# A mixture-of-experts block's second routing loop: tokens four to a partition, whole-row stores, shared experts in pieces, late counts

## The chip, the cores and the metric

The kernel runs on one core of one Trainium2 chip. The metric is device time in microseconds, from the start to the end of one execution; a kernel's time is the median of its runs. A core has TensorE (PE; loading of its weights is shown as PEld), VectorE (DVE), ScalarE (ACT), GpSimd (POOL) and SyncE (SP), each with its own stream of instructions that it works through in order. Engines wait for each other and for transfers through semaphores. DMA transfers are issued by SP, ACT and POOL; an instruction that waits at the head of a stream holds up everything behind it on that engine.

## The reference

The input x has 16 x 512 = 8192 tokens of width 256. Four parts follow each other, each on layer-normalised input and added to x: softmax attention (16 heads), a mixture of experts, a gated linear attention ("forget" attention), and the same mixture of experts again. All is float32. The mixture of experts is:

```python
logits = x.astype(jnp.float32) @ router_w.T          # 64 experts
probs = jax.nn.softmax(logits, axis=-1)
topk_w, topk_ids = jax.lax.top_k(probs, K)           # K = 8
topk_w = topk_w / jnp.sum(topk_w, axis=-1, keepdims=True)
...
pos = jnp.cumsum(onehot, axis=0)[jnp.arange(N), flat_e] - 1
valid = pos < C                                      # C = 128 places an expert
...
g = jnp.einsum('ecd,edf->ecf', xb, w_gate)           # F = 192
u = jnp.einsum('ecd,edf->ecf', xb, w_up)
h = jax.nn.silu(g) * u
y = jnp.einsum('ecf,efd->ecd', h, w_down).reshape(E * C, -1)
...
gu = x @ ws_gate_up                                  # the shared expert, F = 192
sg, su = (gu[:, :SF], gu[:, SF:])
shared = jax.nn.silu(sg) * su @ ws_down
return routed + shared
```

An expert takes its first 128 tokens in token order and drops the others, so the running count of tokens for each expert, over all 8192 tokens in order, decides what is computed.

## The kernel before

The tokens are cut into 16 blocks of 512, a block into four chunks of 128. The first mixture of experts is routed inside the attention's schedule; the second has a loop of its own, in `Block.routed(part, loads=True)`. `Part` holds what both share. The order of the instructions on each engine is written out by hand (`manual_schedule`): an engine works in the order in which the Python code issues.

**The second layer's loop** (L1268 on) runs over b from -4 to 16, each step working on several blocks. In step b it loads block b+4 (SP), chooses the experts of block b, normalises block b+2, transposes block b+1, runs the shared expert's gate and up matmuls and its silu for block b-3, computes router logits and the softmax's numerators for b+1, counts block b, sends the shared expert's result for b-4 through its down matmuls, and takes the moments (mean and variance) for b+3. In detail:

- `normed` (L1530) stores a normalised block's 256 columns to `rows` in DRAM; `choose` (L1575) divides by the softmax's sum (L1579 to L1581), finds the eight largest values of each token (L1589, L1590), makes a mask of them, and stores 64 expert weights per token into the last columns of the same rows. A row of `rows` has 320 values.
- `count` (L1606) transposes the mask with four matmuls (L1611) and copies it out of PSUM (L1613). `added` (L1615) makes the running count with one scan on VectorE (L1619) that begins with the last block's end, and stores it to `counts` in DRAM. `counted` (L1506) reads it back into `cw`, chunks on partitions. The last block goes straight from chip to chip (`straight`, L1512), with two of four DMAs issued by SP and two by ACT.
- `gu` (L1628), `chunk` (L1636) and `silu` (L1647) are the shared expert's first half, `down` (L1677) its second, in two halves; the second half stores the block's result from SP. A matmul in float32 stands as two rows in the trace.
- Expert weights come in pairs of experts, four DMAs a pair (`fetch`, L1483); five pairs are fetched in steps 2 to 6 of the loop, four pieces in a step. Eleven pairs fit on chip.

**The tail.** After the loop `chunks_before` (L1070) reads the counts, and `find` (L1079), driven by `place`, finds each expert's 128 tokens in five pieces of work; the first two calls handle two experts each, the later ones four. Between the pieces stand the shared expert's matmuls for the last blocks. `gather` (L1133) gets the rows of the found tokens by an indirect DMA from POOL.

**The experts.** For each expert the loop at L1359 gathers the rows of six experts ahead, transposes (`turned`), multiplies (`widened`, `narrowed`), and adds the result to `out` or `routed` by an indirect DMA with addition from POOL (L1200), alternating. Weight pieces of later pairs are issued at an even pace. Before it, `part.own.close()` releases the loop's buffers, and `part.slots` zeroes the padding of the new weight buffers on POOL (L1480), which waits for the last readers of the released memory.

At the end `joined` adds `routed` to `out` with eight DMAs of 1 MB.

Of the kernel before, what the change touches and what calls it, by code (L numbers as in the profile page):

```python
# [37 lines left out]
class Block:  # L38
# [131 lines left out]
    def attention(self, x, x1, wqkv, wo, rope, part, later):  # L170
# [14 lines left out]
        with ExitStack() as c:  # L185
# [271 lines left out]
            def each(s):  # L457
# [9 lines left out]
                    if b + far < z - 2 or work not in expert  # L467
# [556 lines left out]
    def routed(self, part, loads=False):  # L1024
# [9 lines left out]
        with ExitStack() as c:  # L1034
# [6 lines left out]
            if loads:  # L1041
                part.look_up("right")
                part.slots(5, "right")
            else:
                part.slots(4, "right")
# [13 lines left out]
            def load(b):  # L1059
                xs[b] = p3.tile([P, CB, D], F32, name="x")  # L1060
                nc.sync.dma_start(
                    out=xs[b], in_=x[ts(b, BLK), :].rearrange("(c p) d -> p c d", p=P)
                )
# [63 lines left out]
            accs = (x, y)  # L1127
# [56 lines left out]
            def narrowed(e):  # L1184
# [3 lines left out]
                for m in range(2):  # L1188
# [12 lines left out]
                    out=accs[e % 2],  # L1201
# [10 lines left out]
            with tc.manual_schedule(  # L1212
# [8 lines left out]
                nb, lag, ahead = self.nblk, 3, 6  # L1221
# [33 lines left out]
                def counts(b):  # L1255
                    part.added(b, stored=b < nb - 1)
                    (part.counted if b < nb - 1 else part.straight)(b)

# [8 lines left out]
                if loads:  # L1267
                    for b in range(-4, nb + 1):  # L1268
# [6 lines left out]
                        run(b - lag, nb, gu)  # L1275
                        run(b - lag, nb, silu)
# [3 lines left out]
                        run(b, nb, counts)  # L1280
                        run(b - 1 - lag, nb, down)
                        run(b + 1, nb, part.exps)
                        run(b + 3, nb, lambda b: part.moments(b, xs[b]))
                        if 2 <= b < 7:
                            fetch(b - 2)
                        if b == nb:
                            chunks_before()
                            place(0, 3)

                    begun, done, z = 5, 0, nb - 1  # L1290
# [3 lines left out]
                    part.gu(z - 1, 0)  # L1294
                    place(2, 1)
                    part.gu(z - 1, 1)
                    place(2, 1)
                    gather_to(3)
                    silu(z - 1)
                    part.down(z - 2, 0)  # L1300
                    part.down(z - 2, 2)
                    place(4, 3)
                    part.gu(z, 0)
                    place(4, 1)
                    part.gu(z, 1)
                    place(4, 1)
                    gather_to(5)
                    silu(z)
                    down(z - 1)
                    down(z)  # L1310
# [43 lines left out]
                part.own.close()  # L1354
                part.slots(part.pairs - len(part.slot), "left")

                rest = [(n, piece) for n in range(begun, E // 2) for piece in range(4)]
                due, last = len(rest), E - 10
                for e in range(done - 2, E):  # L1359
                    if e + ahead > 5:  # L1360
                        run(e + ahead, E, gather_to)
# [4 lines left out]
                    run(e, E, narrowed)  # L1366
                    while rest and (due - len(rest)) * last < due * (e + 1):
# [31 lines left out]
ROOMY = dict(xn=2, xnT=5, pr=2, rest=2, chosen=2, wt=2, cs=2, cum=2, th=2, hT=2, y=2)  # L1399


class Part:
# [6 lines left out]
    def __init__(self, ctx, k, x, y, weights, room, pairs, side):  # L1409
        rw, self.w_gate, self.w_up, self.w_down, ws_gu, ws_down = weights  # L1410
        self.ctx, self.pairs, self.slot, self.ws = ctx, pairs, [], {}
        self.k, self.nc, self.x, self.y, self.room = k, k.nc, x, y, room
# [23 lines left out]
        self.end = 0.0  # L1436
# [3 lines left out]
    def begin(self, queue):  # L1440
        rw, ws_gu, ws_down = self.shared_weights
        nc, T, w = self.nc, self.k.T, self.pools[1]
        self.rw_sb = w.tile([P, KD, E], F32, name="rw_sb")
        queue.dma_start(out=self.rw_sb, in_=rw.rearrange("(k p) f -> p k f", p=P))
# [13 lines left out]
        for i in range(self.room["hT"]):  # L1458
            hT = w.tile([P, 2, BLK], F32, name=f"hT{i}")
            nc.gpsimd.memset(hT[FT:P, 1, :], 0.0)  # L1460
            self.hidden.append(hT)
        for z in (self.rows, self.x, self.y):
            queue.dma_start(out=z[T : T + P, :], in_=self.k.zeros[:, 0 : z.shape[1]])

# [47 lines left out]
    def straight(self, b):  # L1512

        for i in range(CB):
            at, queue = b * CB + i, (self.nc.sync, self.nc.scalar)[i % 2]
            queue.dma_start(out=self.cw[at : at + 1], in_=self.cum[:, ts(i, P)])
# [5 lines left out]
    def here(self, b):  # L1522
        return self.rows[ts(b, BLK), :].rearrange("(c p) d -> p c d", p=P)
# [6 lines left out]
    def normed(self, b, xt):  # L1530
        mv, va, yy = self.mvs.pop(b)
        rstd = self.k.refined(va, yy)
        self.xns[b] = self.tile("xn", [P, CB, D])
        self.k.normed(self.xns[b], xt, mv, rstd, 0)
        self.nc.sync.dma_start(out=self.here(b)[:, :, 0:D], in_=self.xns[b])

    def features(self, b, pool=None):
        xn = self.xns.pop(b)
# [36 lines left out]
    def choose(self, b, piece):  # L1575
        nc, small, pr = self.nc, self.k.small, self.prs[b]
        if piece == 0:
            sm = small.tile([P, CB], F32, name="sm")
            nc.vector.tensor_reduce(sm, pr, AX.X, ALU.add)  # L1579
            nc.vector.reciprocal(sm, sm)  # L1580
            nc.vector.tensor_tensor(  # L1581
                pr, pr, sm.unsqueeze(2).to_broadcast([P, CB, E]), ALU.mult
            )
# [14 lines left out]
        wt = self.tile("wt", [P, CB, E])  # L1598
# [4 lines left out]
        nc.sync.dma_start(out=self.here(b)[:, :, D:ROW], in_=wt)  # L1603
        del self.prs[b], self.tops[b], self.rests[b]

    def count(self, b):  # L1606
# [6 lines left out]
        self.nc.scalar.copy(self.csums[b], cT[0:E, :])  # L1613
# [32 lines left out]

    def silu(self, b, piece):  # L1647
        if piece == 0:
            self.hTs[b] = self.hidden[b % len(self.hidden)]
# [7 lines left out]
    def gate(self, b):  # L1657
# [3 lines left out]
        self.hTs[b] = self.hidden[b % len(self.hidden)]  # L1661
# [15 lines left out]
    def down(self, b, i, pool=None):  # L1677
# [3 lines left out]
        py = self.bank()  # L1681
        for k in range(2):
# [130 lines left out]
```

## Time and profile before

| what | us |
|---|---|
| median of 3 runs (2653.41 to 2655.82) | 2655.49 |
| the profiled execution | 2652.72 |
| its span, first to last instruction | 2650.8 |
| first layer's scatters | 1424.2 to 1643.6 |
| forget attention ends (last addition) | 2131.9 |
| first moments of the second loop | 2142.3 |
| count scans 0, 13 and 15 of the second loop | 2162.23, 2324.39, 2341.03 |
| counts read on chip (L1071) | 2352.08 |
| first scatter of the second layer | 2386.09 |
| last scatter | 2601.34 |
| final addition issued | 2605.76 |

All times in a trace are from the first instruction of the span. The granted clock is TensorE's, 1 being full speed. In a line of the timeline stand the start, the duration, the engine, the source line, the operation, what it writes and reads by the program's names, the shapes, and the number of instructions merged into the line; in brackets the idle time of the engine just before, and what ended it. An engine name with a q is its sequencer issuing a DMA. In a line of waits: who waited for whom, then the total, the number of times and the longest, in us.

### The profile page before, as it was taken

The page shows a single profiled execution, that of the slowest core. Times are in us where ns is not written, and L with a number is a line of the kernel's source. Part 1 is how long each engine was busy: PE and PEld are TensorE (multiplying, and loading weights), DVE is VectorE, ACT ScalarE, POOL GpSimd, SP SyncE. Part 2 cuts the span into 40 slices and gives each one's busy share as a digit, 9 for nine tenths or more (in the row PEclk, how much of TensorE's full clock was granted, in tenths as well). Part 3 has the DMA queues.
Part 4 walks back from the last instruction along what each step waited for, and adds up shares of the span by engine and source line. Part 5 has one row for each costly group of instructions (what it writes and reads, how often), then busy time and mean ns, then how long its engine had stood idle before and what let it go on. Part 6 is the DMA issues. An engine that isn't in the chain of part 4 may idle for free.

```text
span 2650.8 us, 47730 instructions
## 1 busy us (share of the span) xinstructions
PE 2429.4 (92%) x17864; PEld 1514.1 (57%) x17864; DVE 1850.9 (70%) x4677; ACT 1333.9 (50%) x2750; POOL 844.4 (32%) x835
## 2 busy tenths in 40 slices
PE   7999999999999999999997886899999969998871
PEld 3444555555555555555446775567777656667771
DVE  6566677766777676776646664789889869867650
ACT  1566666666666666666542332466666523323330
POOL 3122212222221222212015775332322122117773
PEclk8899999999999999999898898899999969999996
DMA  1000111001110011100158896202111058739987
GB/s 57 1 10 27 35 37 35 14 29 35 37 35 14 29 35 37 36 20 13 35 146 231 222 240 151 82 30 64 54 53 53 22 148 187 177 105 263 246 224 148
DMA packets 210003, 226.47 MB, mean 85 GB/s; under 512 B 34286, under 2 KB 202222, under 8 KB 208750
## 3 DMA queue, kind: packets, MB, share of 16 engines
q1 hardware_dynamic: 180366, 174.43, 22.9%
q0 software_dynamic: 25728, 46.15, 8.8%
q8 instruction: 142, 2.33, 0.4%
q10 hardware_dynamic: 3680, 2.85, 0.3%
q14 instruction: 87, 0.71, 0.1%
HBM read 146.50 MB, written 84.48 MB: 87 GB/s over the span
## 4 chain that ended last, share of the span: by engine, by line
PE 75%; DVE 9%; DMA 8%; issue 3%; POOL 2%; ACT 1%; SPq 0%; POOLq 0%; ACTq 0%; DVEq 0%
PE sc L334 20%; PE sc L384 9%; DMA xe<-rows,token 4%; PE sc L260 4%; PE pb L811 4%; PE sc L1639 3%; PE sc L323 3%; PE sc L843 2%; PE pb L875 2%; PE sc L407 2%; PE sc L304 2%; PE sc L1684 2%; PE pb L920 2%; PE pb L736 2%; PE pb L1165 2%
## 5 line engine op out<-in xcount | busy, mean ns | idle before, releaser
L348 DVE TENSOR_REDUCE mx<-sc 128x1 f32<-128x512 f32 x1024 | 635.1, 682 | 296.2 <-PE sc L334 296.2
L374 ACT ACTIVATE pT<-sc 128x512 f32<-128x512 f32 x1024 | 527.9, 603 | 109.7 <-PE sc L334 109.7
L334 PE MATMUL sc<-qT,kT 17*128 17x512 f32 x2048 | 314.8, 647 | 0.0
L334 PE MATMUL sc<-kT,qT 16*128 16x512 f32 x2048 | 301.8, 610 | 0.3 <-DVE mx L348 0.3
L384 PE MATMUL sc<-pT,v 128*32 128x512 f32 x2048 | 244.3, 620 | 0.0
L104 POOL TENSOR_SCALAR va<-mv 128x4 f32<-128x4 f32 x64 | 14.7, 230 | 704.9 <-DVE mv L98 692.7
L860 DVE SCALAR_TENSOR_TENSOR pT<-sc,of,left 128x256 f32<-128x256 f32 x512 | 204.9, 472 | 21.7 <-PE sc L843 20.4
L334 PEld LDWEIGHTS sc<-kT,qT 16*128 16x128 f32 x2048 | 151.3, 190 | 91.5 <-issue 36.4
L282 POOL TENSOR_TENSOR t<-qk,rope_sb 128x512 f32<-128x512 f32 x62 | 78.8, 1270 | 382.1 <-ACT qk L268 374.5
L334 PEld LDWEIGHTS sc<-qT,kT 17*128 17x128 f32 x2048 | 94.0, 184 | 128.5 <-issue 95.6
L384 PEld LDWEIGHTS sc<-pT,v 128*32 128x32 f32 x2048 | 61.9, 113 | 174.4 <-issue 124.3
L1135 POOL DMA_INDIRECT xe<-rows,token x128 | 130.3, 1018 | 91.0 <-DVE token L1117 38.5
L144 ACT COPY oT<-sc 128x512 f32<-128x512 f32 x64 | 37.5, 586 | 172.7 <-PE sc L384 172.7
L260 PE MATMUL sc<-wqkv_sb,feat 128*128 128x512 f32 x256 | 124.4, 611 | 0.0
L811 PE MATMUL pb<-feat,wqk_sb 128*128 128x512 f32 x256 | 117.7, 593 | 0.0
L1200 POOL DMA_INDIRECT routed<-ye,token x64 | 102.7, 1605 | 40.9 <-DMA routed<-ye,token 10.8
L323 PEld LDWEIGHTS sc<-ident,pad 128*128 128x128 f32 x512 | 55.4, 144 | 104.4 <-ACT pT L374 81.9
L96 DVE BATCH_NORM_STATS2 bn<-x 128x6 f32<-128x256 f32 x256 | 89.0, 410 | 17.1 <-DMA x<-out 13.9
L1599 POOL TENSOR_TENSOR wt<-pr,chosen 128x256 f32<-128x256 f32 x32 | 23.3, 728 | 242.9 <-DVE chosen L1594 218.5
L1639 PE MATMUL sc<-xnT,wsg_sb 128*128 128x512 f32 x192 | 92.5, 608 | 0.0
L323 PE MATMUL sc<-ident,pad 128*128 128x128 f32 x512 | 87.0, 293 | 5.1 <-POOL pad L298 2.8
L290 POOL TENSOR_TENSOR t<-qk,rope_sb 128x256 f32<-128x256 f32 x124 | 90.7, 753 | 0.0
(225 smaller groups left out, 4897.9 us busy)
## 6 DMA issues: line engine op xcount, KB each, us to landing
ws<-in_w_gate SPq DMA_DIRECT2D x64, 384.0 KB
ws<-in_w_up SPq DMA_DIRECT2D x64, 384.0 KB
rows<-xn SPq DMA_DIRECT2D x32, 512.0 KB
routed<-y SPq DMA_DIRECT2D x32, 512.0 KB
ws<-in_w_down SPq DMA_DIRECT2D x64, 256.0 KB
x<-in_x SPq DMA_DIRECT2D x16, 512.0 KB
attended<-x SPq DMA_DIRECT2D x16, 512.0 KB
ws<-in_w_down SPq DMA_DIRECT2D x64, 128.0 KB
```

The costliest lines, as they stand in the source:

```text
L260: nc.tensor.matmul(pq, lhsT=xnTs[b][:, kd, ts(i, P)], rhs=wqkv_sb[:, kd, 0 : 2 * D], start=(kd == 0), stop=(kd == KD - 1),)
L290: eng.tensor_tensor(t2[:, :, lo : lo + HD // 2], qk2[:, :, :, 1 - half], rope_sb[:, i, HD + lo : HD + lo + HD // 2] .unsqueeze(1) .to_broa ...
L323: nc.tensor.transpose(pt[:, ts(i, P)], pads[b % 2][i][:, at : at + 4, :].rearrange("p h d -> p (h d)"), self.ident,)
L334: nc.tensor.matmul(scs[j], lhsT=lhs[at : at + high, ts(i, P)], rhs=rhs[at : at + high, :], start=True, stop=True,)
L348: nc.vector.tensor_reduce(mxs[n][:, j, i : i + 1], sc, AX.X, ALU.max, negate=True)
L374: nc.scalar.activation(pT[:, j, :], sc, AF.Exp, scale=float(HD) ** -0.5)
L384: nc.tensor.matmul(pav[ts(j, HP), :], lhsT=vs[b % 2][:, i, 4 * hg + j, :], rhs=pT[:, j, :], start=(i == 0), stop=(i == CB - 1),)
L811: nc.tensor.matmul(pq, lhsT=wqk_sb[:, kd, ts(m, P)], rhs=xnTs[b][:, kd, :], start=(kd == 0), stop=(kd == KD - 1),)
L860: nc.vector.scalar_tensor_tensor(pTs[n][:, :, ts(s8, HD)], sc[:, :, ts(s8, HD)], of[:, s8 : s8 + 1], here, ALU.mult, ALU.mult,)
L1135: nc.gpsimd.indirect_dma_start(out=xes[e], out_offset=None, in_=rows, in_offset=bass.IndirectOffsetOnAxis(ap=token[:, e : e + 1], axis=0),)
L1200: nc.gpsimd.indirect_dma_start(out=accs[e % 2], out_offset=bass.IndirectOffsetOnAxis(ap=token[:, e : e + 1], axis=0), in_=ye, in_offset=No ...
L1639: self.nc.tensor.matmul(to, lhsT=self.wsg_sb[:, kd, ts(m, P)], rhs=self.xnTs[b][:, kd, :], start=(kd == 0), stop=(kd == KD - 1),)
```

## The change

Only the second layer gets the new layout (`whole=True`); the first layer keeps its order of tokens.

- *Layout.* A partition holds four tokens in a row (`(p c) d -> p c d`) and no longer every 128th token (`(c p) d`), so a block's loads and stores move 4 KB in one piece per partition. `count` copies the counts back into token order by a strided write.
- *Rows whole.* A block's normalised values and its expert weights lie in one buffer of 320 columns, and are stored by one DMA after `choose`. Four such buffers are kept.
- *Softmax sum.* The three VectorE instructions that divide by the sum are removed, in both layers: the chosen weights are divided by their own sum afterwards, so it cancels.
- *Shared experts in pieces.* A block's work has cost 10: the first part (gate and up, 128 wide) 4, the second (64 wide) 2, each half of down 2. `shares` issues pieces up to a quota that grows evenly with b, beginning with block 0 in step 0. 140 of 160 units are due by the end of the loop, 10 before the counts are read, 10 between the placing steps.
- *Counts late.* Block b-1's counts are read back in step b. All four DMAs of the last block are issued by ACT, in both layers.
- *Queues and weights.* The second layer's shared results are stored from ACT. Four pairs of weights are fetched ahead, two pieces in a step from step 3 on; ten pairs fit on chip.
- *Unused here.* Blocks whose shared expert would be put off into the expert loop (`put_off`, `between`, `paid`) are set to none in both layers, so that code issues nothing.

```diff
-                part.slots(5, "right")
+                part.slots(4, "right")
+                part.queue = nc.scalar
...
-                    for b in range(-4, nb + 1):
+                    pieces = []
+                    for n, b in enumerate([*own, None]):
+                        if b is not None:
+                            pieces.append((4, b, first_part, b))
+                        if n > 0:
+                            pieces.append((2, own[n - 1], part.down, own[n - 1], 0))
+                            pieces.append((2, own[n - 1], part.down, own[n - 1], 2))
+                        if b is not None:
+                            pieces.append((2, b, second_part, b))
+                    total, spent = 10 * len(own), 0
+                    begun, done = 4, 0
+                    early = [(n, piece) for n in range(begun) for piece in range(4)]
+
+                    def shares(upto, newest=nb):
+                        nonlocal spent
+                        while pieces and spent + pieces[0][0] <= upto and pieces[0][1] <= newest:
+                            cost, _, work, *args = pieces.pop(0)
+                            spent += cost
+                            work(*args)
+
+                    for b in range(-4, nb):
                         run(b + 4, nb, load)
...
-                        run(b - lag, nb, gu)
-                        run(b - lag, nb, silu)
+                        shares((total - 20) * (b + 1) // nb, b)
                         run(b + 1, nb, part.logits)
                         run(b + 1, nb, part.likely)
                         run(b, nb, part.count)
-                        run(b, nb, counts)
-                        run(b - 1 - lag, nb, down)
+                        run(b, nb, lambda b: part.added(b, stored=b < nb - 1))
+                        if b == nb - 1:
+                            part.straight(b)
+
+                        run(b - 1, nb - 1, part.counted)
                         run(b + 1, nb, part.exps)
                         run(b + 3, nb, lambda b: part.moments(b, xs[b]))
-                        if 2 <= b < 7:
-                            fetch(b - 2)
...
+                        for _ in range(2):
+                            if b >= 3 and early:
+                                part.fetch(*early.pop(0))
+                    shares(total - 10)
+                    chunks_before()
+                    place(0, 3)
+                    shares(total - 8)
                     place(0, 2)
                     gather_to(1)
                     place(2, 3)
...
+                    shares(total - 6)
+                    place(2, 2)
                     gather_to(3)
...
                     place(4, 3)
+                    shares(total - 4)
+                    place(4, 2)
                     gather_to(5)
+                    shares(total)
...
-ROOMY = dict(xn=2, xnT=5, pr=2, rest=2, chosen=2, wt=2, cs=2, cum=2, th=2, hT=2, y=2)
+ROOMY = dict(xn=4, xnT=5, pr=2, rest=1, chosen=2, cs=2, cum=2, th=2, hT=2, y=2)
...
     def straight(self, b):
         for i in range(CB):
-            at, queue = b * CB + i, (self.nc.sync, self.nc.scalar)[i % 2]
-            queue.dma_start(out=self.cw[at : at + 1], in_=self.cum[:, ts(i, P)])
+            at = b * CB + i
+            self.nc.scalar.dma_start(out=self.cw[at : at + 1], in_=self.cum[:, ts(i, P)])
...
+    def tokens(self, z, b):
+        order = "(p c) d -> p c d" if self.whole else "(c p) d -> p c d"
+        return z[ts(b, BLK), :].rearrange(order, p=P)
...
-            sm = small.tile([P, CB], F32, name="sm")
-            nc.vector.tensor_reduce(sm, pr, AX.X, ALU.add)
-            nc.vector.reciprocal(sm, sm)
-            nc.vector.tensor_tensor(
-                pr, pr, sm.unsqueeze(2).to_broadcast([P, CB, E]), ALU.mult
-            )
...
-        nc.sync.dma_start(out=self.here(b)[:, :, D:ROW], in_=wt)
+        if self.whole:
+            nc.sync.dma_start(out=self.here(b), in_=row)
+        else:
+            nc.sync.dma_start(out=self.here(b)[:, :, D:ROW], in_=wt)
...
-        self.nc.scalar.copy(self.csums[b], cT[0:E, :])
+        if self.whole:
+            self.nc.scalar.copy(
+                self.csums[b].rearrange("e (p c) -> e c p", c=CB),
+                cT[0:E, :].rearrange("e (c p) -> e c p", c=CB),
+            )
+        else:
+            self.nc.scalar.copy(self.csums[b], cT[0:E, :])
...
-        part = Part(c, k, out, routed, moe, ROOMY, 11, "left")
+        part = Part(c, k, out, routed, moe, ROOMY, 10, "left", (), True)
```

## The prediction

> **What bounds the kernel now.** The page's engine line says only that TensorE is busy most of the time, so I went to the stretch table, cut at the borders of the stages: second layer's routing loop (2135 to 2341), its tail (to 2386), the experts (to 2601), the final addition.
>
> ```profile
> PE 2429.4 (92%) x17864; PEld 1514.1 (57%) x17864; DVE 1850.9 (70%) x4677; ACT 1333.9 (50%) x2750; POOL 844.4 (32%) x835
> ...
> 2135.00:2160.00 25.00, 12.52 (x52) 10.62 (x52) 13.74 (x61) 2.81 (x6) 6.05 (x10) 0.51 0.59 187
> 2160.00:2183.00 23.00, 16.97 (x66) 13.18 (x67) 22.03 (x81) 5.41 (x12) 5.30 (x9) 0.50 0.75 137
> 2183.00:2260.00 77.00, 73.24 (x331) 50.14 (x330) 71.73 (x240) 24.84 (x48) 15.66 (x24) 0.98 0.85 192
> 2260.00:2341.00 81.00, 74.74 (x344) 53.09 (x343) 73.50 (x247) 25.53 (x48) 15.74 (x24) 0.96 0.64 154
> 2341.00:2386.00 45.00, 42.54 (x177) 29.30 (x176) 23.63 (x53) 11.77 (x24) 10.02 (x13) 0.96 0.33 97
> 2386.00:2601.00 215.00, 179.95 (x1216) 158.92 (x1215) 136.20 (x382) 71.37 (x186) 159.50 (x120) 0.97 0.89 231
> ```
>
> After the stretch's length come PE, PEld, DVE, ACT and POOL, the granted clock, DMA share and GB/s. In the loop VectorE is full and TensorE nearly so; in the tail TensorE alone is. Next the timelines of the two engines through one iteration:
>
> ```profile
> 2217.61 1.04 PE L1545 MATMUL pb<-ident,xn 128*128 128x128 f32 x8
> 2218.49 5.32 PE L1639 MATMUL pb<-xnT,wsg_sb 128*128 128x512 f32 x12
> 2223.64 1.89 PE L1554 MATMUL pb<-rw_sb,xnT 128*128 128x64 f32 x16
> 2225.51 0.63 PE L1611 MATMUL pb<-ident,chosen 128*64 128x128 f32 x4
> 2225.97 3.62 PE L1684 MATMUL pb<-wsd_sb,hT 128*128 128x256 f32 x16
> 2229.43 1.04 PE L1545 MATMUL pb<-ident,xn 128*128 128x128 f32 x8
> ```
> ```profile
> 2219.36 1.27 DVE L1619 TENSOR_TENSOR_SCAN cum<-cs,cum 64x512 f32<-64x512 f32 x1
> ...
> 2222.12 0.38 DVE L1579 TENSOR_REDUCE sm<-pr 128x4 f32<-128x256 f32 x1
> 2222.54 0.18 DVE L1580 RECIPROCAL sm<-sm 128x4 f32<-128x4 f32 x1
> 2222.75 0.42 DVE L1581 TENSOR_TENSOR pr<-pr,sm 128x256 f32<-128x256 f32 x1
> 2223.21 0.23 DVE L1589 MAX8 top<-pr 128x8 f32<-128x64 f32 x1
> ...
> 2231.92 1.27 DVE L1619 TENSOR_TENSOR_SCAN cum<-cs,cum 64x512 f32<-64x512 f32 x1
> ...
> 2262.72 1.41 DVE L96 BATCH_NORM_STATS2 bn<-x 128x6 f32<-128x256 f32 x4 [4.18 <-DMA x<-out]
> ```
>
> From scan to scan VectorE takes 12.56 us, TensorE 11.82 from start to start. The queues' waits show why a load came late once:
>
> ```profile
> SPq L1508 <- DMA counts<-cum: 65.5, 15, 6.5
> ```
>
> SP sits behind each count store; once, at 2258, VectorE paid 4.18 us. In the expert stretch POOL issues without pause: its scatters run from 2386.09 to 2601.34, 3.4 us an expert, both layers alike (1424.2 to 1643.6), so a shift of its start goes to the end whole.
>
> **Prices**, start to start in that iteration. Softmax sum: 2223.21 - 2222.12 = 1.09 us. Silu of a block: 2.81 (first part 1.38, second 1.43). The rest of a VectorE iteration: 12.56 - 1.09 - 2.81 = 8.66. TensorE: transposes 0.87, gate and up 5.15 (first part, 8 of 12 rows, 3.43; second 1.72), each half of down 1.73, router logits 1.73, counting 0.43. The change's cost units are TensorE time: 10 a block, 8.6 us.
>
> **The change, step by step**, against the profiled execution (2652.7 us, span 2650.8; 2.8 under the median 2655.5). I follow the count scans, 0 to 15.
>
> 1. *Start: +3.8.* Scan 0 was at 2162.23. It loses the sum (-1.1) and gains block 0's silu (+2.8): +1.7, if TensorE keeps up. But its 12 new rows stand ahead of block 1's logits, where the clock was granted at one half (2135 to 2183). All at half speed: 10.3 us from 2154.7, logits 3.7, softmax start 0.8, scan near 2169.6: +7.4. In this trace the clock rose 1.3 us after the first wide rows (2182.11); I take about 3 us at half: scan at 2166.
>
>    [...]
>
> 2. *Scans 0 to 13: -6.9.* Before 2324.39 - 2162.23 = 162.2. After, VectorE does 13 x 8.66 = 112.6 and, by the quota 140(b+1)/16, 12 first and 11 second silu parts: 16.6 + 15.7; together 144.9. The 4.18 stall is inside the 162.2 and goes. New: in iterations 4, 5, 12 and 13 the quota puts a half of down(b-1) behind the second part of the same block. It needs that silu, and the logits are queued behind it: after silu come down 1.73, logits 1.73 and a handover 0.2, while VectorE has only 1.38 of other silu before it wants the logits: 2.3, with the late count 2.6 us each, 10.4. So 155.3. Bounds: no stalls -17.3; a stall in all 13, 178.7: +16.5. I take four, from the order of the pieces.
>
> 3. *Scans 13 to 15: +2.3.* No normalisation is left to do; TensorE sets it: (0.87 + 1.73 + 1.72 + 3.43 + 1.73) + handovers 0.4 = 9.9, then 3.45 + 1.72 + 3.43 + 0.43 = 9.0: 18.9 against 16.64.
>
>    Scan 15 thus falls 0.8 us earlier than 2341.03, with 14 units (12.1 us) more of shared work behind it.
>
> 4. *Counts on chip: -2.0.* Before, 2341.03 to the copy at 2352.08: SP issued its two rows at 2347.83. Now ACT issues four (two took 1.19, so 2.4), landing by 8; behind them on ACT wait two y copies and two tanh of the shared work. Ten units of shared work stand ahead; their silu ends near 8.8. I take 9.0 instead of 11.05 (bounds 7.0 and 11).
>
> 5. *Tail: -11.3.* Before, the last down ended at 2379.2, 27.1 after the copy; TensorE was full with 24 units. Now 10 are left, and VectorE's placing steps (0.42 each for two experts, 0.68 for four, as in the rows) come first: tokens of experts 0-1 at +5.0, 2-3 at +8.8, the three first steps of 4-7 to 10.8, silu of block 15 to 12.2, its two halves of down to 15.8. Zeroing of the weight slots on POOL waits for them as before, and first scatter follows the last down by 6.9: +22.7 against +34.0. Bounds: -12.1 (all 14 units) and -7.8 (the second placing ahead of the silu).
>
> 6. *First layer: +1.4.* The change's four count rows from ACT reach it too. Two took 1.45 there and a tanh waited behind them:
>
> ```profile
> 1387.62 1.45 ACTq L1516 DMA_DIRECT2D cw<-cum  x2
> 1389.12 1.07 ACT L1019 ACTIVATE th<-sc 128x512 f32<-128x512 f32 x2 [2.84 <-issue]
> ```
>
>    Its down matmuls and the token search behind them slip by 1.45 (bounds 0 and 1.5). The removed sums save nothing there: TensorE has no gap in the attention, and the last block's counting waits for matmuls.
>
> 7. *At nothing, and under what cover.* Rows stored whole: one issue instead of two, later, but landed some 10 us before the first gather. Loads and stores of four tokens: SP's issues shorten, the loads already come an iteration ahead, and on SP nothing waits in front of them any more except the count store of their own step. y stores on ACT: 16 issues of 0.4 us on an engine busy for 32% of the loop; cover gone, 6.6; POOL keeps its instructions and gets one buffer to zero fewer. Strided count copy: VectorE has 5 us of other work meanwhile; if it doubled, 0.6 each. Late read-back: its gain is the stall in step 2. Weights: one pair fewer ahead, 1.18 MB more in the expert stretch; pair 4 is asked for at expert 0 and read at expert 6, some 16 us. If it isn't hidden, 1.18 MB at 231 GB/s: 5.1.
>
> Sum: 3.8 - 6.9 + 2.3 - 2.0 - 11.3 + 1.4 = -12.7; 2640.0 profiled, 2643 on the median's scale.
>
> **Rivals.**
> - *Waits in every iteration* (slower). TensorE and VectorE are within 0.2 us of each other in a full iteration and 8 banks serve 9 allocations, so a wait may not be made up. 13 stalls instead of four: +23.4, 2666. It decides from nine stalls on. Against: only four iterations have the bad order; elsewhere TensorE may lag 5 us.
> - *No waits*: TensorE is far enough ahead. -10.4: 2632. For: the old loop shows no wait of VectorE on TensorE worth naming. Against: the order is a plain dependency.
> - *Half clock stays until 2183*: an iteration needs 23 us of TensorE, half of 29 us is lost, 14 instead of 3.8: 2653, no change. For: the 0.50 rows. Against: the 1.3 us rise.
> - *Experts pay for the weights*: +5.1, 2648. Against: POOL's pace was no better in the first layer, which has eight pairs ahead.
>
> **How the numbers follow.** Forecast 0.50; no waits (or a still shorter tail) 0.18; experts pay 0.08; half clock 0.12; waits everywhere 0.12. 0.2% is 5.3 us, about what a measurement here can tell from nothing. Faster: the first three and a little of the fourth, 0.78; same 0.11; slower 0.11. The likeliest case alone spans 2636 to 2649; the range goes from 2628 (no waits, best tail) to 2656, leaving out the slow rival.
>
> **What would show it.** Scan to scan 11.5 us in a full iteration; gaps of some 2.4 us before L1566's reduction in four iterations alone; clock at 1 by 2160; SP without waits on count stores; first scatter 34 - 22.7 = 11 us nearer to the copy of counts; the expert stretch still 215 us; first scatter of the first layer 1 us later. It is wrong if the gaps stand in most iterations, if the expert stretch lengthens, or if TensorE rows in the first iterations stay doubled.

## The result and the profile after

The changed kernel takes 2669.69 us (median of 9 runs, 2664.70 to 2676.43), the kernel before 2654.88 us (9 runs, 2651.01 to 2660.31) on the same chip: ratio 1.0061, 95% interval 1.0048 to 1.0074. It is slower by 0.6%, where 2643 us was forecast. The execution that was profiled is the longest of its runs, 2676.43 us with a span of 2674.7, so the two profiles differ by 23.7 us and the medians by 14.8; part of what follows is the one execution, and the experiments say which part.

The stretch table of the changed kernel, cut at the events that also bound rows two to six of the table below, to whole us. After the length come busy PE, PEld, DVE, ACT, POOL, then the granted clock, DMA share and GB/s.

```profile
2135.00:2166.00 31.00, 16.95 (x73) 12.65 (x74) 17.37 (x68) 4.70 (x8) 7.03 (x12) 0.67 0.48 157
2166.00:2342.00 176.00, 153.73 (x687) 109.59 (x686) 138.26 (x476) 58.03 (x100) 33.92 (x52) 0.92 0.59 160
2342.00:2362.00 20.00, 20.00 (x82) 13.34 (x81) 13.37 (x43) 7.73 (x13) 2.68 (x4) 0.98 0.41 134
2362.00:2378.00 16.00, 7.45 (x23) 3.97 (x21) 4.12 (x6) 2.15 (x4) 0.00 (x0) 0.86 0.29 62
2378.00:2403.00 25.00, 22.87 (x102) 17.55 (x103) 15.30 (x40) 5.30 (x13) 10.47 (x13) 0.82 0.27 83
```

The second row is the loop. VectorE is busy for 138.3 of 176 us, and no engine is full: the loop now waits. The fourth row, from the last count scan to the copy of the counts, is worse: 16 us in which TensorE works for 7.5 and VectorE for 4.1.

| stretch, us | before | after | forecast | measured |
|---|---|---|---|---|
| span start to the last addition of forget attention | 2131.9 | 2134.2 | +1.4 | +2.3 |
| from there to scan 0 | 30.4 | 32.1 | +3.8 | +1.7 |
| scan 0 to scan 13 | 162.2 | 175.8 | -6.9 | +13.6 |
| scan 13 to scan 15 | 16.6 | 20.0 | +2.3 | +3.3 |
| scan 15 to the copy of the counts | 11.05 | 15.8 | -2.0 | +4.8 |
| copy to the first scatter | 34.0 | 25.5 | -11.3 | -8.5 |
| first to last scatter | 215.2 | 221.9 | 0 | +6.6 |

The first row says little: over the fourteen profiles of this document forget attention ends between 2118.5 and 2140.5 us, though its code hardly differs.

What VectorE waited for between scan 0 and scan 13 of the changed kernel (who waited for whom: total us, times, longest):

```profile
DVE bn L97 <- DMA x<-out: 14.9, 6, 4.5
DVE mx L1628 <- PE pb L1616: 12.8, 4, 3.8
DVE cum L1689 <- ACT cs L1678: 2.4, 3, 1.1
```

In the same view the kernel before has one line, the 4.2 us of the moments. So there are two new kinds of wait. The second and third lines belong together: they come from the order of the pieces, which the prediction had. The first line, loads that come late, the prediction did not have. SP's own waits in the loop say who made them late:

```profile
SPq L1553 <- DMA routed<-y: 45.3, 4, 14.3
...
SPq L1692 <- DMA routed<-y: 15.0, 1, 15.0
...
SPq L1064 <- DMA routed<-y: 7.5, 1, 7.5
```

SP fetches expert weights (L1553), stores counts (L1692) and loads x (L1064); `routed<-y` is the shared expert's store, which the change moved away from SP, to ACT. SP waits for a transfer that it no longer issues and whose data it doesn't need. One episode, first in ACT's timeline, then in SP's:

```profile
2231.36 0.59 ACT L1756 COPY y<-pb 128x512 f32<-128x512 f32 x1 [0.35 <-PE pb L1767]
2231.98 0.33 ACTq L1758 DMA_DIRECT2D routed<-y  x1
```
```profile
2222.11 0.48 SPq L1565 DMA_DIRECT2D cw<-counts  x1
2236.90 1.10 SPq L1553 DMA_DIRECT2D ws<-in_w_down  x2
2238.04 0.59 SPq L1064 DMA_DIRECT2D x<-out  x1
```

From 2222.6 to 2236.9 SP issues nothing. The semaphores recorded with these instructions give the reason (not a view of the profile, but the trace's own record):

```
2231.98  ACT  routed<-y       signals semaphore 100 when landed
2236.90  SP   ws<-in_w_down   waits for semaphore 100, then signals 100 itself
```

In the whole trace the transfers of SP and of ACT signal the same eight semaphores (100 and 102 to 108), while POOL's signal eight others (111 to 118). In these records an engine that takes a semaphore up again has always waited first for that semaphore's last transfer to land (all 947 reuses by SP and ACT in this trace, all 963 in the one before); the waits are recorded with instructions of the engine's own stream, though none stands in the kernel's source. In the loop of the kernel before, ACT issued none of these transfers between the weights and zeros at its start and the two rows at its end. Now twelve of SP's instructions in the loop wait for a semaphore that a y store from ACT has used last, and ACT issues that store only when the block's down matmuls and their copies are done. So SP, which used to run ahead, is pulled back to the pace of the matmuls plus a store's landing (here 4.9 us, 2231.98 to 2236.88), and the load of block b+4 behind it comes late.

The same thing, sharper, in the stretch after scan 15, in the mixed timeline of the changed kernel:

```profile
2361.99 1.28 DVE L1689 TENSOR_TENSOR_SCAN cum<-cs,cum 64x512 f32<-64x512 f32 x1 [0.86 <-ACT cs L1678]
2363.30 9.48 ACTq L1573 DMA_DIRECT2D cw<-cum  x4
...
2372.88 1.07 ACT L1756 COPY y<-pb 128x512 f32<-128x512 f32 x2 [10.92 <-DMA cw<-cum]
...
2374.98 0.68 DVE L1022 SCALAR_TENSOR_TENSOR th<-th,pb 64x512 f32<-64x512 f32 x1 [11.71 <-ACT th L1021]
...
2377.81 0.21 DVE L1074 COPY after<-cw 64x64 f32<-64x64 f32 x1
```

The prediction gave four issues 2.4 us. They take 9.48, because the fourth signals the same semaphore (108) as the first and waits until that has landed, at 2372.3. Behind it in ACT's stream stand the y copies and the tanh, behind those the silu on VectorE, and behind that the copy of the counts.

The semaphore is not all of it, for the rows themselves land late. In the trace's record of landing signals (again not a view) the first row has twelve of its sixteen by 2366.2 and the last four from 2371.6 to 2372.3; the second and third end like it, by 2372.8. The read-back of block 14's counts, which SP issued at 2359.38, has four signals in all, from 2371.4 to 2372.5. So 10.8 of the 15.8 us pass before three rows and the read-back are on chip, and the shared semaphore can account for at most the 5.0 us after that. That the rows' last signals stand behind the read-back is a reading of these times; no run takes the read-back away.

### The profile page after: what moved, and what is told of

The parts are those of the page before. It is cut to its first block, busy times and chain, and to the rows that moved or that the text cites. A ratio compares the mean times of both kernels' runs of the same rounds, so it can differ in the third digit from the quotient of the medians.

```text
span 2674.7 us, 47602 instructions
## 1 busy us (share of the span) xinstructions
PE 2435.9 (91%) x17864; PEld 1517.7 (57%) x17864; DVE 1818.7 (68%) x4582; ACT 1342.1 (50%) x2750; POOL 843.6 (32%) x834
## 5 line engine op out<-in xcount | busy, mean ns | idle before, releaser
L1204 POOL DMA_INDIRECT routed<-ye,token x64 | 103.1, 1611 | 43.6 <-DMA routed<-ye,token 13.2
L1709 PE MATMUL pb<-xnT,wsg_sb 128*128 128x512 f32 x192 | 88.7, 607 | 0.0
```

The costliest lines, as they stand in the source:

```text
L1204: nc.gpsimd.indirect_dma_start(out=next(accs), out_offset=bass.IndirectOffsetOnAxis(ap=token[:, e : e + 1], axis=0), in_=ye, in_offset=Non ...
L1709: self.nc.tensor.matmul(to, lhsT=self.wsg_sb[:, kd, ts(m, P)], rhs=self.xnTs[b][:, kd, :], start=(kd == 0), stop=(kd == KD - 1),)
```

## The experiments

Theory A: the shared semaphores make the loads late. Theory B: the order of the pieces makes the logits late. Theory C: four DMAs in a row on ACT delay the counts. Every time below is compared with the kernel before in runs on the same chip, as a ratio with its 95% interval. Chips and executions differ, so the table gives times inside the profile from event to event.

| kernel | ratio to before | scan 0 to 13 | loads late | logits late | scan 15 to copy |
|---|---|---|---|---|---|
| changed | 1.0061 (1.0048 to 1.0074) | 175.8 | 14.9 | 12.8 | 15.8 |
| y stored from SP | 1.0005 (0.9986 to 1.0025) | 159.9 | 0 | 12.2 | 15.4 |
| pieces in order | 1.0014 (1.0000 to 1.0027) | 156.3 | 12.4 | 0 | 16.1 |
| last counts on SP and ACT | 1.0045 (1.0025 to 1.0064) | 176.2 | 16.9 | 11.6 | 14.3 |
| all three | 0.9925 (0.9896 to 0.9953) | 143.4 | 0 | 0 | 14.1 |

**One: the shared results stored from SP again.**

```diff
-                part.queue = nc.scalar
```

> The changed kernel with one edit: the second layer's shared results are stored from SP again, not from ACT. Theory A (transfers of SP and ACT take turns on eight completion semaphores, so SP waits for ACT's late stores and the loads behind it come late): VectorE's gaps in the loop that end with the load of x, 14.9 us in the changed kernel's profile, fall under 4 us; the 16.3 us of gaps before the router's softmax in four iterations stay; total 8 to 15 us under the changed kernel, so 2655 to 2662 against its 2670. Theory B (the order of the pieces alone makes the loop slow; late loads only fill time that would be waited anyway): total within 4 us of the changed kernel. Rival C (SP is now held up by ACT's copies as it was before the change): gaps with the load of x stay above 8 us.

2661.01 us, ratio 1.0005: 0.56% is gone with one line. VectorE's waits between scans 0 and 13 in this kernel:

```profile
DVE mx L1627 <- PE pb L1615: 12.2, 4, 4.8
DVE cum L1688 <- ACT cs L1677: 3.7, 4, 1.1
```

The wait for x is gone altogether, the other two stand where they stood. The 15.9 us that the loop lost in length (175.8 to 159.9) are the 14.9 us of that wait and little else.

**Two: no down matmul in the same call as its own silu.**

```diff
+                        fresh = set()
                         while pieces and spent + pieces[0][0] <= upto and pieces[0][1] <= newest:
-                            cost, _, work, *args = pieces.pop(0)
+                            if newest < nb and pieces[0][2] == part.down and pieces[0][1] in fresh:
+                                break
+                            cost, of, work, *args = pieces.pop(0)
+                            if work is second_part:
+                                fresh.add(of)
```

> The changed kernel with one edit: in the loop, a call of shares stops in front of a half of down whose second silu part was issued in the same call, so it comes one iteration later. Theory A+B (own silu in front of the logits): the gaps before the router's softmax in iterations 4, 5, 12 and 13 (16.3 us with the late counts behind them) fall under 4 us in sum; total 8 to 16 us under the changed kernel: 2654 to 2662. If the late loads are the real limit, the gaps move to the load of x, which grow from 14.9 us, and the total falls by less than 5 us.

2657.48 us, ratio 1.0014. Now the other wait is gone, and the loads are late by nearly as much as before (12.4 us, 14.9 in the changed kernel):

```profile
DVE bn L97 <- DMA x<-out: 12.4, 5, 4.8
DVE cum L1694 <- ACT cs L1683: 0.2, 1, 0.2
```

Experiments one and two each remove one wait and leave the other: the two causes are separate.

**Three: the last block's counts from SP and ACT in turn, as before the change.**

```diff
-            at = b * CB + i
-            self.nc.scalar.dma_start(out=self.cw[at : at + 1], in_=self.cum[:, ts(i, P)])
+            at, queue = b * CB + i, (self.nc.sync, self.nc.scalar)[i % 2]
+            queue.dma_start(out=self.cw[at : at + 1], in_=self.cum[:, ts(i, P)])
```

> The changed kernel with one edit: the last block's four count transfers are issued by SP and ACT in turn, as before the change, in both layers. From last scan to the copy of the counts in the second layer 15.8 us go to some 11, in the first layer 8.4 to 8.4 - 1.5; total 4 to 7 us under the changed kernel: 2663 to 2666. Rival: the copy waits for another row's landing, and the total stays within 2 us.

2667.29 us, ratio 1.0045: a little less gain than expected (2663 to 2666), and the interval (1.0025 to 1.0064) takes in the changed kernel's 1.0061, so the times alone don't show a gain. Scan 15 to the copy falls from 15.8 to 14.3 us only: here the read-back of block 14 lands last, 14.25 us after the scan. In the first layer, which runs the same line, the first scatter comes 37.9 us after scan 15 instead of 41.0; it is 37.9 to 38.6 in every kernel here that has the old line, and 41.0 in the three that have the four rows on ACT.

**Four: all three together.**

> All three edits together (stores from SP, no half of down behind its own silu, counts from both queues). If the three causes are separate they add up: 20 to 32 us under the changed kernel, 2638 to 2650, so under the kernel before (2655). If they cover each other, the gain is about that of the largest alone and the total stays at 2655 to 2660. The expert stretch, 221.9 us in the changed kernel against 215.2 before, has had nothing undone and stays at some 220.

2640.66 us, ratio 0.9925 (0.9896 to 0.9953): with three small edits the change is faster than the kernel before by 0.75%. Between scans 0 and 13 VectorE's whole list of waits is

```profile
DVE cum L1693 <- ACT cs L1682: 0.2, 1, 0.2
```

and the stretch takes 143.4 us. The prediction had worked out 144.9 for a loop that only VectorE's own work sets.

**Five: the stores from ACT alone, in the kernel before.** The opposite test of theory A: nothing of the change but the queue.

```diff
-            nc.sync.dma_start(
+            (nc.scalar if self.pairs == 11 else nc.sync).dma_start(
                 out=self.y[ts(b, BLK), :].rearrange("(c p) d -> p c d", p=P),
```

> Another part alone: the kernel before, with the second layer's shared results stored from ACT instead of SP, and nothing else. Theory A (SP and ACT take turns on the same eight completion semaphores, so that SP's next transfer waits for a store that ACT issues late): waits of SP's queue on routed<-y appear in the second loop, which before had 0.2 us of them; moments wait for loads in several iterations, 5 to 15 us in all; ratio 1.002 to 1.006. Rival (only the change's own shape, whole rows and pieces, makes the loads late): no such waits and the time within 3 us of before.

2666.77 us, ratio 1.0071 (1.0053 to 1.0089): this one edit alone costs as much as the whole change. VectorE's waits from scan 0 to scan 13, then SP's in the loop:

```profile
DVE bn L96 <- DMA x<-out: 22.1, 5, 6.2
```
```profile
SPq L1622 <- DMA routed<-y: 52.6, 6, 15.7
SPq L1508 <- DMA counts<-cum: 46.7, 14, 7.7
...
SPq L1535 <- DMA routed<-y: 7.4, 1, 7.4
```

That is more than the 1.002 to 1.006 that was expected, and the loads are late by 22.1 us where 5 to 15 were. SP here still waits behind its count stores too, and the two waits follow each other in its stream.

**Six: the stores from POOL.** With two and three mended, `part.queue = nc.gpsimd`. This tells the shared semaphores from a plainer rival, that a second queue beside SP's slows the loads.

> The version with the order of the pieces mended and the last counts on two queues, but with the shared results stored from POOL instead of SP. In the traces POOL's transfers use eight semaphores of their own. Theory A (the shared semaphores made the loads late): no wait of SP's queue on routed<-y, no wait of the moments for x, scans 0 to 13 near the 143.4 us that stores from SP gave, and the time within 4 us of that version (ratio to before 0.991 to 0.996). Rival (a second queue beside SP's competes for the DMA engines and slows the loads): waits of the moments come back, 8 to 15 us; ratio 0.996 to 1.001.

2631.64 us, ratio 0.9933 (0.9917 to 0.9950), scans 0 to 13 in 143.3 us, no wait of VectorE in that stretch. The rival falls: a second queue with the same bytes does no harm here. POOL's queue may differ from ACT's in more than its semaphores, and no run gave the stores on ACT semaphores of their own; that the semaphores are the cause rests on this run together with SP's recorded waits on them. The runs with the stores from POOL and from SP are equal within their intervals (0.9917 to 0.9950 and 0.9896 to 0.9953).

**Seven: the kernel before without the softmax's sum.** The prediction's main saving by itself.

```diff
-            sm = small.tile([P, CB], F32, name="sm")
-            nc.vector.tensor_reduce(sm, pr, AX.X, ALU.add)
-            nc.vector.reciprocal(sm, sm)
-            nc.vector.tensor_tensor(
-                pr, pr, sm.unsqueeze(2).to_broadcast([P, CB, E]), ALU.mult
-            )
```

> One part of the change alone: the kernel before without the three VectorE instructions of the softmax's sum (in both layers); the result is the same up to rounding, since the sum cancels. The prediction priced them at 1.09 us an iteration of the second loop and at nothing in the first layer. Theory (VectorE sets the old loop, at 12.56 us, and TensorE is next at 11.82): the 13 iterations from scan 0 to scan 13 shrink by 0.7 to 1.1 us each, 162.2 to 148 to 153; the ratio to before is 0.994 to 0.997 (8 to 16 us). Rival (the order of the pieces or the loads hold the loop anyway): scan to scan stays near 12.6 us and the time within 4 us of before.

2647.06 us, ratio 0.9992 (0.9978 to 1.0005): next to nothing. And yet the quiet iterations are 11.5 us from scan to scan instead of 12.56, the 1.09 us that the rows gave. Four others take 15.0, 16.0, 16.5 and 12.2:

```profile
DVE bn L96 <- DMA x<-out: 13.2, 4, 4.9
```
```profile
SPq L1508 <- DMA counts<-cum: 72.5, 15, 6.0
```

The first line is VectorE from scan 0 to 13, the second SP. SP sits behind each count store for 5 us, as it did before. An iteration of 12.56 us left it just enough time; one of 11.5 us doesn't, its loads fall behind, and of the 13 x 1.09 = 14.2 us, 13.2 go back. (The stretch is still 4.8 us shorter, 157.4, since the 4.2 us of late load in the profile before are in its 162.2.) Both ways of the expectation were half right: the iterations shrank as in the theory, and the loads took it back as in the rival.

**Eight: the same, with counts read back one block later.** That is the sum and the late read-back together, in the kernel before.

```diff
                     part.added(b, stored=b < nb - 1)
-                    (part.counted if b < nb - 1 else part.straight)(b)
+                    if b == nb - 1:
+                        part.straight(b)
+                    if b > 0:
+                        part.counted(b - 1)
```

> Two parts of the change together: the kernel before without the softmax's sum, and with block b-1's counts read back in step b instead of block b's. Theory D (alone, the shorter loop overran SP, which sits behind every count store for some 5 us, so that three loads came late and took 12.6 us of the 13 x 1.09 us back; read late, SP doesn't wait): waits on counts<-cum fall from 70.8 us to under 10, no wait of the moments for x over 1 us, 11.5 us from scan to scan throughout, scans 0 to 13 near 145 to 148 us; ratio to before 0.993 to 0.996. Rival (the loads are late for the transfers' own time): waits of the moments stay, 8 us or more; ratio 0.998 to 1.001.

2638.34 us, ratio 0.9936 (0.9915 to 0.9957). SP has no wait on `counts<-cum` left in the loop, VectorE none on loads, and every full iteration takes 11.5 us: scans 0 to 13 in 143.8. The late read-back by itself was not run; in the loop it can only take away a late load, 4.2 us in the profile before and none in experiment nine's, so alone it could hardly give the 0.64%. Two edits without the new layout give nearly all of what the mended change gives, and in the times the two kernels can't be told apart. What the spread shared work adds shows in the tail of the profiles: from the copy of the counts to the first scatter this kernel takes 34.3 us, the one with all three edits 25.4. At the start it costs 2.6 us (29.9 against 32.5 us from forget attention to scan 0).

**Nine: four pairs of expert weights ahead instead of five**, in the kernel before: `slots(4, "right")`, ten pairs, `begun = 4`.

> One more part alone: the kernel before with four pairs of expert weights fetched ahead instead of five, and ten pairs on chip instead of eleven. Theory (weights are landed long before they are read; the expert stretch differs by 216 to 222 us between runs of the very same code in the first layer): the time within 3 us of before, the second layer's stretch from first to last scatter between 214 and 222 us. Rival of the prediction (the experts pay for the pair that isn't fetched ahead): 3 to 6 us slower, with TensorE or ACT waiting for ws in the expert stretch.

Ratio 0.9998 (0.9982 to 1.0014): no price in the time that these runs can tell. In this execution the second layer's stretch from first to last scatter was 222.7 us, and no engine has a wait for `ws` there. The first layer's stretch, whose code is the same in all fourteen profiles, lies between 213.2 and 221.8 us. So the +6.6 us of the table above are of the size by which executions differ. That settles it as not the main cause, not as zero: the second layer's stretch was 215.2 to 219.9 us in four profiles with five pairs (mean 217.4) and 216.7 to 222.7 in ten with four (mean 220.5), so some 3 us of price may stand there unproven.

**Ten to twelve: the wait that stays after scan 15.** In the version with all three edits the copy of the counts still came 14.1 us after scan 15. Its mixed timeline there:

```profile
2330.72 1.28 DVE L1693 TENSOR_TENSOR_SCAN cum<-cs,cum 64x512 f32<-64x512 f32 x1 [0.91 <-ACT cs L1682]
2332.03 1.22 ACTq L1577 DMA_DIRECT2D cw<-cum  x2
...
2335.67 1.14 SPq L1577 DMA_DIRECT2D cw<-cum  x2
...
2336.90 0.44 SPq L1569 DMA_DIRECT2D cw<-counts  x1
...
2344.82 0.22 DVE L1073 COPY after<-cw 64x64 f32<-64x64 f32 x1 [5.97 <-DMA cw<-counts]
```

SP's two rows are issued 3.6 us after ACT's first (in the kernel before, where two queues share the rows in the same way, SP waits at this point for semaphore 100, which ACT's first row signals), and the read-back of block 14, which the change put behind them, lands last of all. Ten moves that read ahead of the count store of its step; eleven also has the last rows on ACT and POOL; twelve has the stores from POOL and the read first, with the rows on SP and ACT.

```diff
+                        run(b - 1, nb - 1, part.counted)
                         run(b, nb, lambda b: part.added(b, stored=b < nb - 1))
...
-                        run(b - 1, nb - 1, part.counted)
```

> The version with all three steps mended, with block b-1's counts read back ahead of block b's count store and not behind it. In that version the read of block 14 was issued after the last block's rows, 6.2 us behind scan 15, landed last, and VectorE, TensorE and ACT all stood still for 6.0 us. Theory: the copy of the counts comes 8 to 11 us after scan 15 instead of 14.1, ended by a transfer of the last block's rows; first scatter 3 to 6 us nearer; ratio to before 0.990 to 0.992. Rival (the last block's own rows land as late): copy at 13 us or more, ratio 0.992 to 0.993.

> The same, with the last block's four rows on ACT and POOL in turn instead of SP and ACT. Theory: POOL's rows need no semaphore that ACT's rows hold, and POOL is idle there, so the copy comes 7 to 10 us after scan 15; ratio 0.989 to 0.992. Rival: POOL's transfers take longer to land than SP's, the copy comes at 12 us or later and the time is that of rows on SP and ACT or more.

> The version that stores the shared results from POOL, with counts read back ahead of the count store. Theory: its 2631.6 less what reading first gives, 3 to 6 us: ratio 0.989 to 0.992, scans 0 to 13 near 143.4. Rival (in the tail POOL's stores then stand ahead of the first gathers): first scatter after the copy of counts later than 26 us, ratio 0.992 to 0.994.

| kernel | ratio to before | scan 15 to copy | copy to first scatter |
|---|---|---|---|
| all three edits | 0.9925 (0.9896 to 0.9953) | 14.1 | 25.4 |
| read first | 0.9928 (0.9906 to 0.9950) | 10.8 | 25.3 |
| read first, last rows on ACT and POOL | 0.9905 (0.9873 to 0.9938) | 9.3 | 24.5 |
| read first, y from POOL | 0.9900 (0.9869 to 0.9930) | 10.1 | 24.5 |

In the profile the copy moves as expected, by 3.3 to 4.8 us. In the times that is 0.15% and less than the intervals: ten by itself shows no gain. The last two have the lowest ratios, but their intervals take in that of the version with all three edits. All four beat the kernel before, the last by 1.0% (2625.32 us, 6 runs, 2616.92 to 2629.71).

## Why the prediction was wrong

It was wrong in sign. By its own steps:

- **Step 7, y stores from ACT at nothing: the step that failed.** It priced the issue on ACT (6.6 us if the cover were gone) and held that the loads stay on time, on the ground that "on SP nothing waits in front of them any more except the count store of their own step". What it never asked is what SP's transfers wait for besides data. The kernel before could have shown it: SP's two last rows wait until 2347.8 for the semaphore (100) of ACT's first, issued at 2342.33; step 4 names SP's time, 2347.83, and doesn't ask what it waited for. The cost is 14.9 us in the profile and 0.56% in the times by experiment one, and 0.71% alone by experiment five.
- **Step 2, four bad iterations: right in place, mis-sized.** The waits stand in iterations 4, 5, 12 and 13 and nowhere else, but with the four of the scan behind them (the last lies just past the window shown) they are 16.3 us, not 10.4. The first of them, TensorE and then VectorE:

```profile
2208.64 1.94 PE L1767 MATMUL pb<-wsd_sb,hT 128*128 128x256 f32 x6 [3.95 <-DVE hT L1023]
2210.37 3.51 PE L1616 MATMUL pb<-rw_sb,xnT 128*128 128x64 f32 x16
```
```profile
2209.41 0.69 DVE L1023 SCALAR_TENSOR_TENSOR hT<-th,pb 128x512 f32<-128x512 f32 x1
2213.92 0.42 DVE L1628 TENSOR_REDUCE mx<-pb 128x4 f32<-128x256 f32 x1 [3.83 <-PE pb L1616]
```

  The chain is the one described: silu, down, logits, reduction. But the sixteen router rows take 3.51 us and not 1.73 (start to start in the prediction's own iteration they take 1.87), and the stretch table around them shows why (the clock is the number after POOL's busy time):

```profile
2204.00:2208.60 4.60, 0.68 (x3) 0.19 (x1) 4.37 (x13) 0.00 (x0) 1.34 (x2) 1.00 1.12 201
2208.60:2212.00 3.40, 3.36 (x15) 3.08 (x15) 1.37 (x2) 0.59 (x1) 0.00 (x0) 0.66 0.69 276
2212.00:2214.00 2.00, 2.00 (x11) 1.96 (x11) 0.08 (x1) 0.00 (x0) 0.00 (x0) 0.50 0.05 20
...
2224.00:2229.00 5.00, 4.01 (x31) 3.85 (x32) 2.92 (x6) 0.83 (x2) 0.00 (x0) 1.00 0.21 17
```

  While TensorE stood for 3.95 us its clock was granted in full; the work after it ran at one half. In the next iteration TensorE stood for 1.14 us only, the clock stayed at 1.00 (last line), and VectorE's gap is 1.88. A stall was priced as if the matmuls behind it ran at full speed. Of TensorE's four waits for that silu (3.95, 1.14, 5.73 and 2.11 us) all but the second had the clock fall to 0.50 within them or soon after (it stood there from 2210 to 2216, from 2319 to 2322 and from 2337 to 2342); how long a stall must be for that, no run shows. The prediction followed the clock at the loop's start and didn't ask what its own stalls would do to it. The VectorE term itself was good: 144.9 forecast for a loop without waits, 143.4 measured in the version with all three edits. 144.9 + 14.9 + 16.3 = 176.1, against 175.8: the two failed terms account for the whole stretch.
- **Step 1**, +3.8 forecast, +1.7 measured, the lower of its two values, which the step gave for a TensorE that keeps up. The 3 us at half speed behind the +3.8 were the author's estimate and no run shows them. The clock rose sooner:

```profile
2138.00:2158.00 20.00, 8.95 (x34) 7.40 (x35) 9.85 (x44) 2.55 (x5) 3.78 (x8) 0.50 0.53 173
2158.00:2166.00 8.00, 8.00 (x40) 5.25 (x39) 7.52 (x26) 2.15 (x3) 2.35 (x3) 0.97 0.20 82
```

  The first wide rows began at 2156.56; from 2158.5 on the clock was up, 1.9 us later. Half speed, which held until 2183 before, costs nothing here that shows, and that rival is out.
- **Step 3**, +2.3 forecast, +3.3 measured, 20.0 us in length; every other kernel with the new layout takes 18.9 to 19.1, as forecast (18.9).
- **Step 4 failed, in part for the same reason as step 7**: 9.0 forecast, 15.8 measured, outside its bounds of 7.0 and 11. The four issues on ACT were priced at 2.4 us and took 9.48; the rows were to land by 8, and three of them were on chip only after 10.8. The read-back of block 14, which came to stand last, was not in the step at all; with both mended the stretch is 9.3 to 10.8.
- **Step 5**, 22.7 forecast, 25.5 measured: sign and most of the size right (34.0 before). It is 24.4 to 26.3 in the other kernels with the new layout, so the chain was some 2 to 4 us short. Where they lie was not followed up; in the changed kernel the clock stood at 0.50 from 2374 to 2387, which the step did not price.
- **Step 6**, +1.4 forecast for the first layer. ACT's later tanh (1.0 us) is as forecast; by the first scatter it is 3.0. Experiment three shows that all 3.0 come with the four rows on ACT. How the other 2.0 come about stays open: no single wait accounts for them, but TensorE's clock falls to one half there 15.8 us after scan 15 and is back at 26.1 in the changed kernel, and at 12.0 and 22.3 us in the kernel before. The +2.3 of the table, near this step's +1.4, is no confirmation, since that row moves by far more between executions.
- **The rivals.** The experts' weights cost nothing that could be measured. The slower rival (a wait for TensorE in every iteration) is out: four iterations, as taken. That the measured time lies close to its 2666 us is chance. No rival had late loads, since they were excluded by the sentence in step 7. A plain bound would have let them in: the one load wait of before, 4.18 us, in half of the iterations is 27 us, and that is more than the whole forecast gain.

The forecast for the change as it was meant was near: with the three edits the kernel's median (4 runs) stands 13.7 us under that of the kernel before; the sum was -12.7. The ratio puts it at 20 us, with an interval of 12 to 28. That it is near is in part luck, as the loop gained 12 us more than forecast and scan 15 to the copy some 5 less.

## What to carry to other kernels

When a transfer is moved to another engine's queue, look up in the trace which completion semaphores the two queues signal: here SP and ACT share eight, so that SP, which ran ahead, was tied to ACT, which issued late; the price was waits of up to 15.0 us for data that SP didn't need. When a busy engine gets shorter, ask at once what was only just in time beside it: the softmax's sum was worth nothing that could be measured alone, and 0.6% once the wait on SP that the slower loop had hidden was gone too. And mend one step at a time from the change's side as well as add one at a time from the kernel before: here 0.6% slower and 0.75% faster lay three short edits apart.

## What was not expected

- In the traces of both kernels SP's and ACT's transfers signal one set of eight semaphores (100 and 102 to 108), POOL's another (111 to 118). A store that was issued from ACT and landed in 4.9 us held SP's next transfer, and all that stood behind it, for 14.3 us; the longest such wait was 15.0.
- ScalarE's copy of the counts out of PSUM with a strided write takes 1.07 to 1.12 us where the plain one took 0.57 to 0.58. It lies beside other work and cost nothing that shows in the mended loop.
- Executions of the very same code differ by more than most terms of the sum: the first layer's expert stretch by 8.6 us over fourteen profiles. A difference of a few us between two profiles needs timed runs before it is given a cause.
